# Five more block products by seven multiplications in an fp32 two-layer network: q·G in the first attention, the out projection in the second

## The chip, the cores and the metric

One Trainium2 chip, one core of it. The time is device microseconds (us) of one execution. The kernel before takes 990.49 us, the median of 3 runs (990.44 to 990.85). The profile is of one further execution, which took 988.88 us.

## The reference

Two transformer layers in fp32, for a batch of 2 sequences of 1024 tokens with 512 channels; a layernorm with a residual stands around each of the four parts.

```
# layer 0, linear attention: q, k = elu(x W) + 1; v = x Wv
out = einsum('bhtd,bhde,bht->bhte', q, k^T v, 1 / (q . sum k))
x   = layernorm(x + out @ Wo.T)
# layer 0, feed-forward: weights of 4 bits, unpacked and scaled; y / rms(y)
x   = layernorm(x + ffn4(x))
# layer 1, gated linear attention, 16 heads that share q and k
go  = o @ Wog.T + x @ Wig.T
o   = o * rsqrt(mean(o*o)) * g_norm_w * (go * sigmoid(go))
x   = layernorm(x + o @ Wo.T)
# layer 1: a router takes the top 512 of each 1024 tokens, an MLP adds to these
x   = layernorm(scatter_add(x, top, sigmoid(score) * mlp(x[top])))
```

The first attention is computed as x + q·G, where q already carries the weight 1/(q · sum k), and G (512 x 512 for a sequence) is (kᵀx) Wv, masked to the heads, times Wo.

## The kernel before

**Tiling.** Tokens go in four blocks ("blk" 0 to 3) of 512; blocks 0 and 1 are sequence 0, blocks 2 and 3 sequence 1. A block is four row tiles of 128 tokens. Stages of the span: layer-0 attention 6.7 to 238 us, the 4-bit feed-forward 238 to 552, the gated attention 552 to 782, the routed MLP 789 to 972, then stores.

**Products by seven.** A block product of 512 x 512 by 512 x 512 is 16 matmuls of 128x512 if it is done whole. `by_seven` (L307) cuts both operands into 2 x 2 and needs seven products of half size (the Strassen-Winograd form), each of 4 matmuls of 128x256, with sums on VectorE: S1 = A21 + A22, S2 = S1 - A11, S3 = A11 - A21, and A12 - S2 of one operand; T1 to T4 of the other (`sums_of_weights`, L297). One PSUM bank, `grow`, takes product after product on top of one another, and a reader takes its value after each; the bank `side` does so for two. Before the change this form serves the projections q and k (L307), the gate of the second attention (`gate`, L1078) and the down products of the feed-forward (L679).

**Stage 1.** The loop `for b in range(B)` (L518) runs `run(products, *others)` (L490): the generator of seven products of the next projection, and between its steps lists of other steps: `add_xk` (kᵀx, L360), `values` and `G_rows` (L411, L427: G, copied from PSUM by VectorE and ScalarE in turn), `turned` (L434: the transposes of a row tile of q), `add_o` (L440), `unpack_some` (unpacks 4-bit weights on VectorE, L237 and L238) and `split_some` (L458: the split of x into a high and a low part for stage 2). `behind()` and `last_pe` pin TensorE's order to the order in which these steps are written; a scheduler orders the other engines' queues, each of which runs in order. `add_o(blk, i)` issues four matmuls of 128x512 into a bank, `ao` (L445), adds it to x (L453) and takes the row statistics (L188, L189); after the fourth row tile, GpSimd (POOL) applies the layernorm (L183). `weigh` (L396; L400 to L406) applies the weight to q, and is called from within `by_seven` through `ready`.

**Stage 3.** For each block, `attend` (L1016) computes o and the sums that gate's products need (L1056, L1057), `gate` computes go in seven products: (L1089), written from PSUM by ScalarE's copies and VectorE's adds, then Silu; the result is `u`, transposed, in a tile `uT` of its own for each block. `finish(blk - 1)` (L1123) is the out projection of the block before, 16 matmuls of 128x512 (L1133), four operations that add it to x, the row statistics, the layernorm and the router's scores (L1146). `route` turns the scores of a sequence into row numbers (L1163), and rows are fetched by them ("picked", "xs") for stage 4. TensorE's order in stage 3 is the scheduler's.

**The start.** L138 to L142 issue the loads of Wk on SP's DMA queue and of the first block of x transposed (`x0T`) on ScalarE's queue, the first of them in small pieces (k = 0: three pieces of x0T, of 128, 128 and 256 columns, and two halves of Wk). The first projection (L474) multiplies them as they land.

Of the kernel before, what the change touches and what calls it, by code (L numbers as in the profile page):

```python
# [10 lines left out]
F32 = mybir.dt.float32  # L11
# [62 lines left out]
def body(ctx: ExitStack, tc: tile.TileContext, a: dict, out: bass.AP):  # L74
# [63 lines left out]
    for k in range(KC):  # L138
        for half in ((slice(0, 256), slice(256, 512)) if k == 0 else (slice(0, 512),)):
            nc.sync.dma_start(out=Wk[:, k, half], in_=a["WkT"][k * P : (k + 1) * P, half])  # L140
        for part in ((slice(0, 128), slice(128, 256), slice(256, 512)) if k == 0 else (slice(0, 512),)):
            nc.scalar.dma_start(out=t[:, k, part], in_=src[:, k, part])  # L142
# [154 lines left out]
    def sums_of_weights(w, rooms):  # L297

        B11, B12, B21, B22 = (w[:, 2 * e : 2 * e + 2, 256 * o : 256 * o + 256] for e in range(2) for o in range(2))
        T1, T2, T4 = rooms  # L300
        for dst, x, y in ((T1, B12, B11), (T2, B22, T1), (T4, B21, T2), (B12, B22, B12)):
            nc.vector.tensor_sub(dst, x, y)
        return T1, T2, B12, T4
# [91 lines left out]
    def weigh(blk, t):  # L395

        for r in range(2):
            x = pairs_of["q", blk][t][:, r]
            e = wk.tile([P, C], F32, tag="e", name="qk")
            nc.vector.tensor_mul(e, x, ksum_of[blk // 2])  # L400
            z = sp.tile([P, 16], F32, tag="z", name="z", bufs=2)
            nc.vector.tensor_reduce(z, e.rearrange("p (h d) -> p h d", d=32), AX.X, ALU.add)
            nc.vector.tensor_scalar_add(z, z, 1e-6)
            nc.vector.reciprocal(z, z)
            x3 = x.rearrange("p (h d) -> p h d", d=32)
            nc.vector.tensor_mul(x3, x3, z.unsqueeze(2).to_broadcast([P, 16, 32]))  # L406

    vkm_of, qT, parts = {}, {}, []
# [23 lines left out]

    def turned(blk, i):
        with behind():  # L434
            pt = transposed(pairs_of["q", blk][i // 2][:, i % 2], "qTp", acc_bank)
        last_pe[0] = last_turned[0]
        t = qT[blk, i] = wk.tile([P, KC, P], F32, tag="qT", name="qT")
        nc.scalar.copy(t.rearrange("p k t -> p (k t)"), pt)

    def add_o(blk, i):  # L440

        ao = acc_bank("ao")
        with behind():
            for k in range(KC):
                ins = nc.tensor.matmul(  # L445
                    ao, qT[blk, i][:, k], G_of[blk // 2][:, k], start=k == 0, stop=k == KC - 1
                ).ins
        last_pe[0] = ins
        x = x_t[blk][:, i]
        if i == 0:  # L450
            mv_of[blk] = sp.tile([P, 4, 2], F32, tag="mv", name="mv")
        mv = mv_of[blk]
        nc.vector.tensor_add(x, ao, x)  # L453
        row_stats(mv[:, i], x)
        if i == 3 and blk < NB - 1:
            layernorm(x_t[blk], mv, by=nc.gpsimd)
# [48 lines left out]
    def some_o(blk, *part):  # L505
        return [lambda i=i: add_o(blk, i) for i in part]
# [6 lines left out]
    def q_products(blk):  # L513
        return by_seven(xT[blk], Wq, Ts["q"], S_rooms, pairs_of.setdefault(("q", blk), []), lambda t: weigh(blk, t))

    step = lambda f, *x: [lambda: f(*x)]

    for b in range(B):  # L518
        i, j = 2 * b, 2 * b + 1
        if b:  # L520
            run(
                k_products(i),
                turns(1, 0, 1),
                some_o(1, 0) + turns(1, 2) + job(1) + some_o(1, 1) + turns(1, 3) + job(1),
                some_o(1, 2) + job(1), some_o(1, 3) + job(1), job(2),
            )
# [3 lines left out]
        else:  # L530
# [7 lines left out]
            q_products(i), [],  # L538
            some_xk(j, 0, 1) + job(1), some_xk(j, 2) + step(spread_ksum, b) + job(1), some_xk(j, 3) + job(1 + b),
        )  # L540
        if b == 0:
# [4 lines left out]
            q_products(j),  # L546
            step(values, b),
            turns(i, 0, 1) + job(1 - b),
            step(G_rows, b) + split[0] + job(1 - b),
            some_o(i, 0) + turns(i, 2) + split[1] + some_o(i, 1) + turns(i, 3) + job(1 - b),  # L550
            some_o(i, 2) + split[2] + some_o(i, 3),
# [3 lines left out]
    rings["free"] = rings["mm"]  # L555
    for more in turns(3, 0, 1) + split[3] + some_o(3, 0) + turns(3, 2) + some_o(3, 1) + turns(3, 3) + some_o(3, 2, 3):
        more()
# [496 lines left out]
    def other_sums(blk):  # L1054
        x, o = xT[blk], oT[blk]
        nc.vector.tensor_sub(x[:, :, 256:], o[:, :, 256:], x[:, :, 256:])  # L1056
        nc.vector.tensor_sub(T4, T2, o[:, :, :256])  # L1057

    banks = []
# [18 lines left out]
    def gate(blk):  # L1078

        u = uT[blk] = place_w(3, "uT")  # L1080
# [4 lines left out]
        def product(w, b, half):  # L1085
            ps = acc_bank("go")
            for m in range(2):
                for k in range(KC):
                    nc.tensor.matmul(  # L1089
                        ps[:, 256 * m : 256 * m + 256],  # L1090
                        w[:, k, m],
                        b[:, k, 256 * half : 256 * half + 256],
                        start=k == 0,
                        stop=k == KC - 1,
                    )
            return ps.rearrange("p (m t) -> p m t", m=2)

        def end(e):
            half = u.rearrange("p (m e) t -> p m e t", e=2)[:, :, e]
            nc.scalar.activation(half, half, AF.Silu)  # L1100
            for m in range(2):
                f = 2 * m + e
                ins = nc.vector.scalar_tensor_tensor(
                    u[:, f], oT[blk][:, f], gw[:, f : f + 1], u[:, f], ALU.mult, ALU.mult
                ).ins
            return ins

        nc.scalar.copy(c11, product(gA11, x, 0))
        yield
        nc.scalar.copy(c22, product(gS1, T1, 0))  # L1110
        yield
        p2 = product(gA12, oT[blk], 0)
        nc.vector.tensor_add(c12, c11, product(gS2, T2, 0))
        yield nc.vector.tensor_add(c11, c11, p2).ins
        nc.vector.tensor_add(c21, c12, product(gS3, x, 1))
        nc.vector.tensor_add(c12, c12, c22)
        yield nc.vector.tensor_add(c22, c22, c21).ins
        nc.vector.tensor_add(c12, c12, product(gS4, oT[blk], 1))
        yield end(0)
        nc.vector.tensor_sub(c21, c21, product(gA22, T4, 0))  # L1120
        yield end(1)

    def finish(blk):  # L1123

        mv = sp.tile([P, 4, 2], F32, tag="mv", name="mv")
# [3 lines left out]
        if blk == 3:  # L1129
            steps = [(0, 0), (0, 1), (1, 0), (1, 1), (0, 2), (0, 3), (1, 2), (1, 3)] + steps[8:]  # L1130
        for i, n in steps:
            k = (0, 2, 1, 3)[n]
            nc.tensor.matmul(ao[i], uT[blk][:, k, i * P : (i + 1) * P], W1o[:, k], start=n == 0, stop=n == 3)  # L1133
# [4 lines left out]
        power = layernorm(x_t[blk], mv)  # L1138
# [8 lines left out]
        return power, ins  # L1147
# [304 lines left out]
    for blk in range(NB):  # L1452
        sum2 = attend(blk)
        if blk == 0:
            plain_gate(0, False)
        else:
            o_sum(blk)
            _, scored = finish(blk - 1)
            gating = gate(blk)
            for _ in range(2):  # L1460
                next(gating)
# [123 lines left out]
```

## Time and profile before

| what | value |
|---|---|
| median of the runs | 990.49 us (990.44 to 990.85) |
| the profiled execution | 988.88 us |
| its span | 987.1 us |
| granted TensorE clock, mean | 0.998 |
| DMA | 48.84 MB, mean 49 GB/s |

The profile follows one execution from its first to its last instruction, the span. PE is TensorE's matmuls, PEld its weight loads, DVE VectorE, ACT ScalarE, POOL GpSimd, SP the engine whose DMA queue takes most loads. A matmul in fp32 leaves two records. A row of the kind `L445 PE ao<-G,qT 128x512 x128 | 57.3, 593` gives line, engine, output and inputs by the program's names, shape, number of records, busy time in us, and the mean duration of one in ns; the records of neighbouring matmuls overlap, so what a matmul takes is read from a run of them on the chain of waits. The list of waits names the line of an engine that stood idle, what released it, and us in total, times, and the longest. In a timeline the first two numbers are start and duration in us.

### The profile page before, as it was taken

What the parts mean: (1) busy time and instruction counts of PE and PEld (TensorE: products, weight loads), DVE (VectorE), ACT (ScalarE), POOL (GpSimd) and SP (SyncE); (2) the same over time, 40 slices, a digit from 0 to 9 for tenths busy, and PEclk for the clock granted to TensorE, in tenths of its full rate; (3) what the DMA queues carried; (4) which work ended last, traced back from release to release, by engine and by line L of the source; (5) the groups of instructions that cost most, each with busy time, mean ns of one, the idle gap of its engine ahead of it and who ended that gap; (6) DMA issues with size and microseconds to landing.
All of it is one profiled execution on the core that took longest, in us unless ns stands there. A gap on an engine that the chain in (4) does not pass through costs nothing.

```text
span 987.1 us, 11453 instructions
## 1 busy us (share of the span) xinstructions
PE 972.1 (98%) x4253; PEld 745.1 (75%) x4253; DVE 683.3 (69%) x1291; ACT 288.4 (29%) x490; POOL 300.2 (30%) x276
## 2 busy tenths in 40 slices
PE   9999999999999999999999999999999999999996
PEld 6667666756888888888889655776768688888885
DVE  3568877867975686686672465466798795789644
ACT  2244333333542272263240432132220123220000
POOL 1110452004887265575565022002032011000022
PEclk9999999999999999999999999999999999999999
DMA  9632212100000000000020500000004302140011
GB/s 332 200 91 79 72 53 93 37 0 1 1 1 1 1 1 0 2 11 1 1 86 1 220 4 1 1 1 1 1 33 139 128 17 70 43 171 1 1 43 43
DMA packets 25979, 48.84 MB, mean 49 GB/s; under 512 B 4685, under 2 KB 6733, under 8 KB 25412
## 3 DMA queue, kind: packets, MB, share of 16 engines
q1 hardware_dynamic: 23139, 42.85, 13.1%
q0 software_dynamic: 1920, 4.22, 1.1%
q10 hardware_dynamic: 864, 1.05, 0.3%
q8 instruction: 33, 0.54, 0.2%
q14 instruction: 23, 0.18, 0.1%
HBM read 39.70 MB, written 10.52 MB: 51 GB/s over the span
## 4 chain that ended last, share of the span: by engine, by line
PE 84%; issue 8%; DVE 4%; POOL 2%; ACT 1%; DMA 1%; POOLq 0%; ACTq 0%; DVEq 0%
PE P L679 12%; PE yp L1329 9%; PE hp L1250 9%; PE gatep L632 8%; PE upp L632 8%; PE ao L445 6%; PE xk L367 6%; PE grow L316 5%; PE P L316 4%; PE ao L1133 3%; PE go L1089 2%; PE lp L595 1%; PE P L688 1%; PE kp L474 1%; PE up L1006 1%
## 5 line engine op out<-in xcount | busy, mean ns | idle before, releaser
L181 POOL TENSOR_TENSOR rs<-rs,table 128x4 f32<-128x4 f32 (+1 forms) x21 | 18.9, 902 | 327.9 <-DVE rs L180 327.6
L643 DVE SCALAR_TENSOR_TENSOR gate<-gatep,scale,gate 128x512 f32<-128x512 f32 x123 | 91.4, 743 | 7.4 <-PE gatep L632 6.9
L643 DVE SCALAR_TENSOR_TENSOR up<-upp,scale,up 128x512 f32<-128x512 f32 x112 | 83.1, 742 | 0.2
L632 PE MATMUL gatep<-x1Th,wgu 128*128 128x512 f32 x176 | 72.7, 413 | 0.0
L632 PE MATMUL upp<-x1Th,wgu 128*128 128x512 f32 x176 | 69.7, 396 | 0.0
L632 PE MATMUL gatep<-x1Tl,wgu 128*128 128x512 f32 x176 | 69.6, 395 | 0.0
L632 PE MATMUL upp<-x1Tl,wgu 128*128 128x512 f32 x176 | 69.5, 395 | 0.0
L679 PE MATMUL P<-wdn,h 128*128 128x256 f32 x256 | 60.5, 379 | 0.0
L832 POOL TENSOR_TENSOR h<-up,gate 128x512 f32<-128x512 f32 x30 | 38.6, 1287 | 70.4 <-ACT gate L831 65.3
L637 ACT ACTIVATE gate<-gatep,scale 128x512 f32<-128x512 f32 x41 | 28.3, 691 | 106.8 <-PE gatep L632 106.8
L445 PE MATMUL ao<-G,qT 128*128 128x512 f32 x128 | 57.3, 593 | 0.0
L1133 PE MATMUL ao<-W1o,uT 128*128 128x512 f32 x128 | 55.6, 592 | 0.0
L679 PEld LDWEIGHTS P<-wdn,h 128*128 128x128 f32 x256 | 48.5, 190 | 6.7
L1037 POOL TENSOR_TENSOR sum<-sum,sq 128x512 f32<-128x512 f32 x12 | 18.2, 1517 | 107.6 <-issue 83.7
L1133 PEld LDWEIGHTS ao<-W1o,uT 128*128 128x128 f32 x128 | 24.0, 190 | 28.7 <-issue 27.5
L188 DVE BATCH_NORM_STATS2 st<-x 128x6 f32<-128x512 f32 x64 | 42.7, 682 | 0.8
L367 PE MATMUL xk<-pair,x 128*128 128x512 f32 x96 | 42.7, 592 | 0.0
L445 PEld LDWEIGHTS ao<-G,qT 128*128 128x128 f32 x128 | 23.8, 190 | 24.3 <-issue 23.9
L632 PEld LDWEIGHTS upp<-x1Th,wgu 128*128 128x128 f32 x176 | 33.0, 188 | 9.3 <-DVE up L643 1.1
L632 PEld LDWEIGHTS upp<-x1Tl,wgu 128*128 128x128 f32 x176 | 33.1, 188 | 7.6
L632 PEld LDWEIGHTS gatep<-x1Th,wgu 128*128 128x128 f32 x176 | 33.1, 188 | 7.4 <-issue 0.3
L632 PEld LDWEIGHTS gatep<-x1Tl,wgu 128*128 128x128 f32 x176 | 33.1, 188 | 7.1
(405 smaller groups left out, 2239.5 us busy)
## 6 DMA issues: line engine op xcount, KB each, us to landing
pk<-in_gu SPq DMA_DIRECT2D x16, 352.0 KB, 3.7
x<-in_x SPq DMA_DIRECT2D x4, 1024.0 KB, 13.1
w<-in_w SPq DMA_DIRECT2D x1, 4096.0 KB, 16.1
xs<-picked SPq DMA_DIRECT2D x4, 1024.0 KB, 5.0
out<-x SPq DMA_DIRECT2D x4, 1024.0 KB, 4.3
w<-in_w SPq DMA_DIRECT2D x4, 1024.0 KB, 6.3
x0T<-in_xT SPq DMA_DIRECT2D x3, 1024.0 KB, 7.2
pk<-in_dn SPq DMA_DIRECT2D x11, 256.0 KB, 3.3
```

Source lines behind the costliest of these rows:

```text
L188: nc.vector.bn_stats(st, x)
L316: ins = nc.tensor.matmul(ps[:, 256 * r : 256 * r + 256], a[:, k, r * P : (r + 1) * P], b[:, k], start=first and r == 0 and k == 0, stop=k ...
L367: ins = nc.tensor.matmul(acc_of[b][c], x_t[blk][:, i, c * P : (c + 1) * P], pairs_of["k", blk][i // 2][:, i % 2], start=blk % 2 == 0 and i ...
L445: ins = nc.tensor.matmul(ao, qT[blk, i][:, k], G_of[blk // 2][:, k], start=k == 0, stop=k == KC - 1).ins
L632: ins = nc.tensor.matmul(ps, wgu[:, k, at * P : (at + 1) * P], x[:, k], start=x is parts[0], stop=x is parts[1]).ins
L637: nc.scalar.activation(acc, ps, AF.Copy, scale=s)
L643: last = nc.vector.scalar_tensor_tensor(acc, ps, s, acc, ALU.mult, ALU.add).ins
L679: last_p[0] = nc.tensor.matmul(cut, x(j)[:, r], w[:, j], start=j == 0, stop=j == NP - 1 and tail is None).ins
L832: hm = nc.gpsimd.tensor_mul(h.chunk(f), up, gate).ins
L1133: nc.tensor.matmul(ao[i], uT[blk][:, k, i * P : (i + 1) * P], W1o[:, k], start=n == 0, stop=n == 3)
L1250: nc.tensor.matmul(ps[:, 256 * j : 256 * j + 256], w[:, k, 2 * g + j], x[:, k], start=k == 0, stop=k == 1)
L1329: nc.tensor.matmul(ps[:, 256 * r : 256 * r + 256], x(r, j), w(j), start=j == 0, stop=j == NJ - 1)
```

## The change

1. q·G of blocks 0, 1 and 2 goes by seven products (`o_products`), in place of four `add_o`; block 3 stays whole (`whole_o`). q transposed is one tile for a block. The sums of G are made in `G_rows`, for each sequence. Each product is added to x by VectorE; `grow` takes four products and `side` two. The row statistics and POOL's layernorm come behind the last product.
2. In `run`, q's and k's products are interleaved with the new steps in another distribution; `weigh` of the second block of a sequence is no longer called by `by_seven` but placed among the steps; the four splits of block 0 are spread over q(3)'s products.
3. The out projection of blocks 0 and 1 in stage 3 goes by seven products (`finish_by_seven`), interleaved with gate's products; blocks 2 and 3 stay with `finish`. The sums of its weight are made once (`sums_of_W1o`), those of u for each block (`sums_of_u`). `scored_rows` holds what came after the out projection.
4. `gate` lets its products accumulate in PSUM, in two banks, in place of four of VectorE's adds, and ScalarE copies or applies Silu straight from the bank; all blocks share one `uT`, and TensorE's order there is pinned by `last_3`.
5. The third piece of x0T at the start is issued on SP's queue.

The diff, cut to its core:

```diff
-            nc.scalar.dma_start(out=t[:, k, part], in_=src[:, k, part])
+            (nc.sync if part.start == 256 else nc.scalar).dma_start(out=t[:, k, part], in_=src[:, k, part])
...
     def G_rows(b):
...
+        TG[b] = sums_of_weights(G_of[b], rooms), pieces_of(room[:, 3])
...
+    def o_products(blk):
+
+        A11, A12, A21, A22 = (qT[blk][:, 2 * e : 2 * e + 2, 256 * t : 256 * t + 256] for t in range(2) for e in range(2))
+        G = G_of[blk // 2]
+        B11, _, B21, B22 = (G[:, 2 * e : 2 * e + 2, 256 * o : 256 * o + 256] for e in range(2) for o in range(2))
+        (T1, T2, T3, T4), S1 = TG[blk // 2]
+        S2 = pieces_of(wk.tile([P, 512], F32, tag="qS", name="qS", bufs=1))
+
+        def product(ps, a, b, first, t, o):
+
+            with behind():
+                for r in range(2):
+                    for k in range(2):
+                        ins = nc.tensor.matmul(
+                            ps[:, 256 * r : 256 * r + 256], a[:, k, r * P : (r + 1) * P], b[:, k],
+                            start=first and r == 0 and k == 0, stop=k == 1, skip_group_check=True,
+                        ).ins
+            last_pe[0] = ins
+            x = x_t[blk][:, 2 * t : 2 * t + 2, 256 * o : 256 * o + 256]
+            nc.vector.tensor_add(x, x, ps.rearrange("p (r c) -> p r c", r=2))
+
+        nc.vector.tensor_add(S1, A21, A22)
+        nc.vector.tensor_sub(S2, S1, A11)
+        nc.vector.tensor_sub(A21, A11, A21)
+        grow = acc_bank("grow")
+        product(grow, A11, B11, True, 0, 0)
+        yield
+        product(acc_bank("P2"), A12, B21, True, 0, 0)
+        yield
+        product(grow, S2, T2, False, 1, 0)
+        nc.vector.tensor_sub(A12, A12, S2)
+        yield
+        side = acc_bank("P7")
+        product(side, A21, T3, True, 1, 1)
+        yield
+        product(grow, S1, T1, False, 1, 1)
+        yield
+        product(side, A22, T4, False, 1, 0)
+        yield
+        product(grow, A12, B22, False, 0, 1)
+        yield
+        mv = mv_of[blk] = sp.tile([P, 4, 2], F32, tag="mv", name="mv")
+        with tc.issue_after(weighed[0]):
+            for i in range(4):
+                row_stats(mv[:, i], x_t[blk][:, i])
+            layernorm(x_t[blk], mv, by=nc.gpsimd)
+        yield
...
         if b:
             run(
                 k_products(i),
-                turns(1, 0, 1),
-                some_o(1, 0) + turns(1, 2) + job(1) + some_o(1, 1) + turns(1, 3) + job(1),
-                some_o(1, 2) + job(1), some_o(1, 3) + job(1), job(2),
+                turns(1, 0, 1) + job(1), job(1),
+                turns(1, 2, 3) + some_o(1, 1) + job(1), some_o(1, 2) + job(1), some_o(1, 5) + job(1),
             )
...
         run(
-            q_products(j),
+            q_products(j, lambda t: None),
             step(values, b),
-            turns(i, 0, 1) + job(1 - b),
-            step(G_rows, b) + split[0] + job(1 - b),
-            some_o(i, 0) + turns(i, 2) + split[1] + some_o(i, 1) + turns(i, 3) + job(1 - b),
-            some_o(i, 2) + split[2] + some_o(i, 3),
+            turns(i, 0, 1) + split[0] + job(1 - b),
+            step(G_rows, b) + split[1] + turns(i, 2, 3) + job(1 - b),
+            some_o(i, 2) + split[2] + some_o(i, 1) + job(1 - b),
+            step(all_free) + some_o(i, 1) + step(weigh, j, 0) + split[3] + some_o(i, 3) + step(weigh, j, 1) + some_o(i, 1),
         )
...
     def gate(blk):
...
-        nc.scalar.copy(c11, product(gA11, x, 0))
-        yield
-        nc.scalar.copy(c22, product(gS1, T1, 0))
-        yield
-        p2 = product(gA12, oT[blk], 0)
-        nc.vector.tensor_add(c12, c11, product(gS2, T2, 0))
+        one, two = acc_bank("go"), acc_bank("go")
+        nc.scalar.copy(c11, product(one, gA11, x, 0, True))
+        yield
+        p5 = product(two, gS1, T1, 0, True)
+        yield
+        nc.scalar.copy(c22, p5)
+        yield
+        nc.scalar.copy(c12, product(one, gS2, T2, 0, False))
+        p2 = product(acc_bank("go"), gA12, oT[blk], 0, True)
         yield nc.vector.tensor_add(c11, c11, p2).ins
-        nc.vector.tensor_add(c21, c12, product(gS3, x, 1))
-        nc.vector.tensor_add(c12, c12, c22)
-        yield nc.vector.tensor_add(c22, c22, c21).ins
-        nc.vector.tensor_add(c12, c12, product(gS4, oT[blk], 1))
+        p7 = product(one, gS3, x, 1, False)
+        yield nc.vector.tensor_add(c22, c22, p7).ins
+        nc.vector.tensor_add(c12, c12, product(two, gS4, oT[blk], 1, False))
         yield end(0)
-        nc.vector.tensor_sub(c21, c21, product(gA22, T4, 0))
+        nc.scalar.activation(c21, product(one, gA22, T4, 0, False), AF.Silu)
+        nc.scalar.activation(c22, c22, AF.Silu)
         yield end(1)
...
+    def finish_by_seven(blk, u, w):
+
+        (A11, A12, A21, A22), (S1, S2) = u
+        (B11, B21, B22), (T1, T2, T3, T4) = w
+
+        def product(ps, a, b, first, s, o):
+
+            with tc.issue_after(last_3[0]) if last_3[0] else contextlib.nullcontext():
...
+            last_3[0] = ins
+            for r in range(2):
+                i = 2 * s + r
+                x = x_t[blk][:, i, 256 * o : 256 * o + 256]
+                nc.vector.scalar_tensor_tensor(
+                    x, ps[:, 256 * r : 256 * r + 256], inv[blk][:, i : i + 1], x, ALU.mult, ALU.add
+                )
...
-            _, scored = finish(blk - 1)
             gating = gate(blk)
-            for _ in range(2):
-                next(gating)
+            if blk < 3:
+                finishing = finish_by_seven(blk - 1, sums, W1o_sums)
+                for _ in range(2):
+                    next(finishing)
+                    next(gating)
+                next(finishing)
+                scored = scored_rows(blk - 1)
+            else:
+                scored = finish(blk - 1)
+                for _ in range(2):
+                    next(gating)
+            next(gating)
```

## The prediction

> **What bounds the kernel now.** I read the page first: the busy shares, the tenths and the chain that ended last by engine.
>
> ```profile
> span 987.1 us, 11453 instructions
> PE 972.1 (98%) x4253; PEld 745.1 (75%) x4253; DVE 683.3 (69%) x1291; ACT 288.4 (29%) x490; POOL 300.2 (30%) x276
> PE   9999999999999999999999999999999999999996
> DVE  3568877867975686686672465466798795789644
> PE 84%; issue 8%; DVE 4%; POOL 2%; ACT 1%; DMA 1%; POOLq 0%; ACTq 0%; DVEq 0%
> ```
>
> TensorE is busy in 98% of the span, in every slice but the last. It is idle for 987.1 - 972.1 = 15 us, most of it at the start and the end. Second, what TensorE waits for, the whole list:
>
> ```profile
> PE dp L989 <- DVE last L974: 1.5, 2, 1.2
> PE ep L942 <- ACT l L931: 1.3, 1, 1.3
> PE hp L1250 <- ACT row L1218: 1.1, 1, 1.1
> PE idle L285 <- DVE ones L281: 1.0, 1, 1.0
> PE rp L1163 <- DVE score L1146: 0.9, 1, 0.9
> PE kp L474 <- DMA x0T<-in_xT: 0.3, 1, 0.3
> PE mp L1043 <- POOL sum L1037: 0.3, 1, 0.3
> ```
>
> That is 6.4 us in all. No bank that `by_seven` fills (`grow`, `P`) is in it: products that accumulate into one bank, with a reader in between, cost TensorE nothing today. So a saved matmul saves its own time, as far as the other engines keep up. Third, therefore, the stretches that the change touches, cut out as windows: q·G of blocks 0 and 1, q·G of block 2 with the splits, and the out projections of blocks 0 and 1. Columns: length, then busy time of PE, PEld, DVE, ACT, POOL, granted clock, DMA share, GB/s.
>
> ```profile
> 84.50:133.50 49.00, 49.00 (x173) 30.44 (x172) 38.55 (x78) 19.34 (x31) 10.75 (x6) 1.00 0.22 66
> 184.40:238.20 53.80, 53.80 (x219) 34.19 (x217) 39.66 (x84) 18.36 (x31) 8.63 (x5) 1.00 0.00 1
> 612.60:643.00 30.40, 30.40 (x155) 21.92 (x154) 15.69 (x29) 5.59 (x9) 4.65 (x4) 1.00 0.00 1
> 673.60:710.00 36.40, 36.40 (x139) 23.95 (x138) 25.34 (x46) 6.49 (x11) 6.14 (x5) 1.00 0.00 1
> ```
>
> PE is full in all four at full clock; VectorE is idle for 10.4, 14.1, 14.7 and 11.1 us. The spare VectorE time is what the change spends.
>
> **1. Five blocks in seven products.** From the chain, one `by_seven` product and one whole out projection; from the groups, a weight load of such a product:
>
> ```profile
> 97.51 1.73 PE P L316 x8
> ```
>
> ```profile
> 612.74 13.73 PE ao L1133 x32
> ```
>
> ```profile
> L316 PEld LDWEIGHTS P<-Wq,b 128*128 128x128 f32 x32 | 6.1, 190 | 0.8
> ```
>
> A matmul leaves two records. 32 records of 512 columns take 13.73 us (0.429 each); a 256-column product takes 8 records, 1.73 us (0.216 each). Whole: 13.73. Seven products: 7 x 1.73 = 12.09 (1.727 unrounded). Saved: 1.64 a block, and for the three q·G and two out projections **-8.2 us**. The order of instructions says the same: 80 matmuls of 512 columns fewer, 140 of 256 more.
>
> A rule speaks against it: the Trainium skill, "TensorE: Matmul & The Clock Gate", The mechanism, has it that a weight load overlaps matmuls in flight only where its row group differs. These loads fill the array, and a block goes from 32 to 56 of them. In series, a block would cost 56 x (0.190 + 0.216) = 22.7 instead of 32 x (0.190 + 0.429) = 19.8 us: +2.9, so +14.6 in five. But the row has eight records with eight loads of 0.190 in 1.73 us, which leaves no room for a load in series: the loads are hidden. The measurement decides: -8.2.
>
> **2. VectorE in q·G of blocks 0 and 1.** An operation of 512 elements lasts 0.68 us and follows the last at 0.60. Each block gains 3 sums of q, one A12 - S2 and 7 adds of products, and loses 4 adds (L453): 7 x 0.60 = +4.2. The four sums of G add 2.4. Two blocks: +10.8. The four row statistics of block 1 (2.8) now come behind its last add. So, until that add, 38.55 + 10.8 - 2.8 = 46.6 us of work; 0.8 of it can't be closed up, where VectorE waits for ScalarE's exponentials. VectorE ends at 84.5 + 47.4 = 131.9. TensorE alone would end at 133.5 - 2 x 1.64 = 130.2. VectorE becomes the bound by 1.7 and a hand-over of 0.2: **+1.9**. By place: the third product needs S2, which stands behind the copies and sums of G (0.5); the third product of block 1 likewise (0.9); a continuation on `side` (0.5). Queued behind a waiting product are the next products of q, for TensorE's order is pinned. Bounds: 0 (the scheduler's order hides all) to 3.3 (all taken back).
>
> Does POOL slow these sums? The layernorm of block 0 (L183, 9.5 us) now runs beside the three sums of block 1.
>
> ```profile
> 116.62 0.97 DVE L238 TENSOR_SCALAR pk<-pk 128x704 int32<-128x704 int32 x1
> ...
> 121.89 0.68 DVE L340 TENSOR_TENSOR rw<-x0T,rw 128x512 f32<-128x512 f32 x1
> ```
>
> ```profile
> 614.53 2.29 DVE L1056 TENSOR_TENSOR x2T<-oT,x2T 128x1024 f32<-128x1024 f32 x1
> ```
>
> Both of the first run beside L183. The Trainium skill, "GPSIMD Engine Reference", Specifications, says that VectorE contends with GpSimd where it has two SBUF inputs. L1056 bears it out beside L1037 (2.29; its like L1057 alone has 1.21), L340 doesn't beside L183 (0.68, as always; the integer L238 takes 0.97 for 0.52). By the rule three sums take about 0.6 more each and the two blocks save 1.8 us less; by L340 nothing. The sums are L340's kind beside the same POOL instruction: nothing, with 1.8 in the range.
>
> **3. q·G of block 2, the splits and block 3.** VectorE: 39.66 + 4.2 + 2.4 = 46.3 us of work in 53.8 - 1.6 = 52.2: it fits. Spots remain where split 3's copies and the last product come close: **+0.4** (0 to 1.5). The layernorm of block 2 starts after its last product; the first gate/up matmuls need only the splits of block 0, so its cover is stage 2. Moving `weigh` out of q's products costs nothing while VectorE has this room; `all_free` only opens banks earlier.
>
> **4. Out projection and gate, blocks 0 and 1.** VectorE per block: 14 operations of 128x256 at 0.40 (L1375's kind, 0.48 long) for 4 of 512, 14 x 0.40 - 4 x 0.60 = +3.2, and 4 sums, +2.4; W1o's sums, +2.4 once; four gate adds fewer in each of three blocks, -2.4 each. Two blocks and W1o: 11.2 + 2.4 - 4.8 = +8.8, against 14.7 + 11.1 us idle. ScalarE takes the copies and Silu straight from PSUM, with idle 24.8 and 29.9 of the windows. A continuation waits for VectorE to read the bank: 0.2 to start, 0.69, 0.15 back, 1.04 us, under the 1.73 of the product in between; here gate's products stand in between too. I take **+0.3** (0 to 1.5). W1o lands at 557.3 (5.5 us after its issue); by the order of instructions its sums stand in VectorE's queue where it is at 558.3, 50 us ahead of their use. That is 1.0 us of cover: later than that, all of VectorE's queue, attention's first operations, would wait with them. The scores of block 1 come later behind the row statistics, but what is fetched by them landed at 748.7 and is first used at 764.5: 16 us of cover, so nothing; without it, `rp L1163` (0.9) would grow by the delay of about 2.
>
> **5. The load.** The third piece of the first xT, 128 x 256 values, went third on ScalarE's queue (issued at 1.64, landed at 6.69; TensorE waits 0.3 for it at 6.73). On SP's queue it is third too, behind two halves of Wk: 0, with -0.3 to +0.3. All that SP issues behind it (three more pieces of Wk, x, the next xT, the shift, the table) comes one small load later; no wait in the list is for one of these, and ScalarE's own later pieces come one earlier.
>
> Sum: -8.2 + 1.9 + 0.4 + 0.3 + 0 = **-5.6 us**. The profiled execution took 988.88 (span 987.1 and 1.78 around it), so span 981.5 and 983.3; the median of the runs, 990.49, is 1.61 above the profiled one, so 984.9.
>
> **The rivals.**
> B: VectorE's order hides everything but 0.6: 990.49 - 7.6 = 982.9. For it: before, no product waits for VectorE, and by the windows three of four stretches have room. Against: 47.4 us of work for 45.7.
> C: VectorE takes back most: POOL's slowing (1.8) and the upper bounds of parts 3 and 4 in halves (1.7 more): -2.1, 988.4. For: the VectorE row has 8s and 9s there already. Against: L340.
> D, slower: a ping-pong between TensorE and VectorE. All 20 continuations on a PSUM bank (four in each of five blocks) wait for an add, the add behind q queued VectorE operations: 1.04 + 0.60 q - 1.73 each. It decides where a continuation costs over 8.2 / 20 = 0.41, at q = 1.8. At q = 2.5: 20 x 0.81 = 16.2, net +8.0: 998.5. Against: `by_seven` has three such continuations in every block and none waits; and where VectorE isn't full, such queues don't stand. The windows have it idle for a fifth to a half.
> E: the change doesn't do what it says, as the loads aren't hidden: 990.49 + 14.6 = 1005.1; excluded by the 1.73 us row.
>
> **How the numbers follow.** A measurement of this kernel tells about 0.2% (2.0 us) from no change. A (the sum, 983.5 to 986.8) has 0.54, B 0.22, C 0.17 (986.8 to 991), D 0.06, E 0.01. Faster than 988.5: A, B and half of C, 0.84; within: the rest of C, 0.09; slower: 0.07. The range runs from 982.0 (all of 8.2 kept and 0.3 of the load) to 989.0; D, E and a part of C, about 0.15, are left out.
>
> **What would show it.** Right: q·G and out products at 1.73 with loads of 190 ns; new waits of TensorE for VectorE's S2 and on `grow` or P7 in stage 1, about 2 us; VectorE without gaps from about 85 to 132; stage 1 ending some 2.5 us earlier, the stretch with the out projections 3 us. Wrong: products of 256 columns above 1.73; waits on each continuation, in stage 3 too; sums of over 1 us beside L183; a longer wait for xT at the start; or a new wait for the scores or for the rows fetched by them.

## The result and the profile after

The changed kernel takes 985.68 us, the median of 6 runs (984.94 to 985.81), against 990.47 (989.04 to 990.85, 6 runs) before: ratio 0.9953, 95% interval 0.994 to 0.9965, so 4.8 us or 0.47% faster. The forecast was 984.9 with a range of 982.0 to 989.0.

```profile
PE 967.1 (98%) x4373; PEld 768.5 (78%) x4373; DVE 697.6 (71%) x1340; ACT 290.3 (30%) x496; POOL 302.9 (31%) x276
```

By the two profiled executions the gain is only 987.1 - 983.8 = 3.3 us. Of the 1.5 us between this and 4.8, 0.8 lie in the first 20 us: TensorE reaches the second block's first product (`grow L316`) at 18.86 us in the profile of before and at 19.64 in that of after, and this differs from execution to execution, as the first experiment shows.

```profile
18.86 1.89 PE L316 MATMUL grow<-Wk,x0T 128*128 128x256 f32 x8
```

```profile
19.64 1.89 PE L316 MATMUL grow<-Wk,x0T 128*128 128x256 f32 x8
```

From that product to the end of the span the two take 968.24 and 964.16 us: **4.08 us less**. This time, from that product to the end of the span, is called the "rest" below and given for every kernel; it can be read to 0.1 us. The remaining 0.7 between 4.08 and the medians' 4.8 can't be placed, as only one execution of each kernel has a profile.

What TensorE waits for, in the profile of after (total, times, longest):

```profile
PE ep L1008 <- ACT l L997: 1.8, 2, 1.3
...
PE gatep L698 <- DVE x1Tl L212: 0.6, 1, 0.6
PE up L1072 <- DVE decay L1057: 0.4, 1, 0.4
PE x2Tp L197 <- ACT e L1009: 0.4, 1, 0.4
...
PE grow L462 <- DVE x L468: 0.3, 1, 0.3
```

Against the list of before, `ep` has a second wait of 0.5, and the other four lines are new. One is in q·G of block 0 (`grow`), one at the entry into stage 2 (`gatep`), three in stage 3. Where the saved 8.2 us went is read by taking the same TensorE work in both traces and asking how much earlier it starts, with the start of the rest set equal:

| stretch | saved on TensorE | seen in the traces | taken back | predicted |
|---|---|---|---|---|
| q·G of blocks 0 and 1 (to the next k product, 133.52 and 131.71) | 3.28 | 2.59 | 0.7 | 1.9 |
| block 2, splits, entry into stage 2 (to stage 2's first products `P`) | 1.64 | -0.23 | 1.9 | 0.4 |
| stage 3 (to `hp`, 780.0 before) | 3.28 | 1.71 | 1.6 | 0.3 |
| all | 8.20 | 4.07 | 4.1 | 2.6 |

The time of a product is as forecast. Here are the weight loads of q·G, then three products from block 0's stretch, the middle one with S2 (columns: start, duration):

```profile
L462 PEld LDWEIGHTS P<-G,wdn 128*128 128x128 f32 x32 | 6.1, 190 | 0.8
```

```profile
91.25 1.89 PE L462 MATMUL P<-G,wdn 128*128 128x256 f32 x8
93.41 1.99 PE L462 MATMUL grow<-wdn,qS 128*128 128x256 f32 x8 [0.27 <-DVE x L468]
95.24 1.89 PE L316 MATMUL grow<-Wq,rw 128*128 128x256 f32 x8
```

Starts without a wait are 1.73 us apart (the printed duration includes the last matmul's tail), loads take 190 ns as before. The product with S2, block 0's third, starts 0.43 late (91.25 + 1.73 = 92.98), of which the list of waits has 0.27, and its successor another 0.10: here a stall costs more than its entry. It waits not for S2, which is done at 92.15, but for the add that reads `grow` after the first product and stands behind S2 in VectorE's queue:

```profile
92.67 0.69 DVE L468 TENSOR_TENSOR x<-x,grow 128x512 f32<-128x512 f32 x1
```

A second delay, of 0.18 with its successor's, at 103.96 (block 0's seventh product) is in no list. The stretch by busy time (length, PE, PEld, DVE, ACT, POOL):

```profile
84.50:131.70 47.20, 46.94 (x223) 39.80 (x222) 46.93 (x91) 20.07 (x33) 14.77 (x8) 1.00 0.25 74
```

VectorE is busy for 46.93 of 47.20 us: full, as forecast. At the entry into stage 2:

```profile
217.98 0.50 PE L698 MATMUL gatep<-x1Th,wgu 128*128 128x512 f32 x1 [0.57 <-DVE x1Tl L212]
...
240.54 0.50 PE L698 MATMUL gatep<-x1Th,wgu 128*128 128x512 f32 x1
...
241.20 0.50 PE L698 MATMUL upp<-x1Th,wgu 128*128 128x512 f32 x1
```

A pair of gate/up matmuls (high and low part) takes 0.47 us where nothing holds it; here two pairs start 0.66 apart, and VectorE's operations that empty their banks (L709) follow each other at 0.66 too. That lasts from 239.4 to 242.9 and costs about 1.2 us, in no line of the list.

### The profile page after: what moved, and what is told of

Read it like the earlier page. It is cut to its first block, busy times and chain, and to the rows that moved or that the text cites. A ratio compares the mean times of both kernels' runs of the same rounds, so it can differ in the third digit from the quotient of the medians.

```text
span 983.8 us, 11753 instructions
## 1 busy us (share of the span) xinstructions
PE 967.1 (98%) x4373; PEld 768.5 (78%) x4373; DVE 697.6 (71%) x1340; ACT 290.3 (30%) x496; POOL 302.9 (31%) x276
## 5 line engine op out<-in xcount | busy, mean ns | idle before, releaser
L181 POOL TENSOR_TENSOR rs<-rs,table 128x4 f32<-128x4 f32 (+1 forms) x21 | 20.3, 967 | 301.3 <-DVE rs L180 301.0
L709 DVE SCALAR_TENSOR_TENSOR gate<-gatep,scale,gate 128x512 f32<-128x512 f32 x123 | 91.5, 744 | 7.4 <-PE gatep L698 6.9
L709 DVE SCALAR_TENSOR_TENSOR up<-upp,scale,up 128x512 f32<-128x512 f32 x112 | 83.2, 743 | 0.2
L1463 PE MATMUL yp<-w,h 128*128 128x256 f32 x168 | 37.7, 379 | 0.0
L745 PE MATMUL P<-T,S 128*128 128x256 f32 x160 | 35.8, 379 | 0.0
L1463 PEld LDWEIGHTS yp<-w,h 128*128 128x128 f32 x168 | 31.9, 190 | 4.3
L1377 ACT ACTIVATE h<-h,b 128x512 f32<-128x512 f32 x28 | 18.4, 713 | 57.2 <-DVE h L1401 34.6
```

Of the source, the lines that this page charges most:

```text
L181: power = nc.gpsimd.tensor_tensor(rs[:, :n], rs[:, :n], const("mhalf")[:, :n], ALU.pow).ins
L709: last = nc.vector.scalar_tensor_tensor(acc, ps, s, acc, ALU.mult, ALU.add).ins
L745: last_p[0] = nc.tensor.matmul(cut, x(j)[:, r], w[:, j], start=j == 0, stop=j == NP - 1 and tail is None).ins
L1377: nc.scalar.activation(x, x, AF.Gelu_apprx_tanh, bias=b1[:, f : f + 1])
L1463: nc.tensor.matmul(ps[:, 256 * r : 256 * r + 256], x(r, j), w(j), start=j == 0, stop=j == NJ - 1)
```

## The experiments

Each kernel is given with its rest, from `grow L316`'s first start to the end of the span (before 968.24, changed 964.16).

### The load at the start

```diff
 # before, with:
-            nc.scalar.dma_start(out=t[:, k, part], in_=src[:, k, part])
+            (nc.sync if part.start == 256 else nc.scalar).dma_start(...)
```

> The kernel before with only the third piece of x0T moved to SP's queue. The prediction put this at 0 (-0.3 to +0.3). Theory M, from the two traces: TensorE enters the second block's products 0.78 us later (19.64 for 18.86), so the move costs about 0.8 us: 991.3 for 990.5. Rival L: the start differs from execution to execution (the profiled execution of before was 1.6 us under its median, and the change is 4.8 us by the medians but 3.3 by the spans), and the move makes the common case better: 989.0 or less.

Measured 989.55 us against 989.93 (27 runs) for before, ratio 0.9994 (0.9986 to 1.0003). The start is at 19.44, the rest 968.26.

> The changed kernel with the third piece of x0T back on ScalarE's queue. Theory M: 0.8 us less than the changed kernel, 984.9. Rival L: more than the changed kernel, 986.4 or above. By the prediction: the same 985.7.

Measured 985.85 us, ratio to before 0.9954 (0.9941 to 0.9968); start 19.95, rest 964.15. So the move is worth nothing that can be measured, as predicted; theory M took one execution's start for the kernel's, and L falls too. With the load back, and against this before of 27 runs, the medians give 985.85 - 989.93 = -4.08, as the rest does. In the four profiles with the piece on ScalarE's queue the start lies at 18.86, 19.63, 19.95 and 20.50; in the ten with it on SP's (the changed kernel's among them) between 19.44 and 20.32. The first projection shows two causes. These lines are from the profile of before, then from that of the kernel with stage 3 alone changed (below), then from that of the changed kernel:

```profile
4.51 1.89 PE L474 MATMUL kp<-Wk,x0T 128*128 128x256 f32 x8
6.73 12.29 PE L474 MATMUL kp<-Wk,x0T 128*128 128x256 f32 x32 [0.33 <-DMA x0T<-in_xT]
```

```profile
4.61 2.94 PE L474 MATMUL kp<-Wk,x0T 128*128 128x256 f32 x8
8.37 12.29 PE L474 MATMUL kp<-Wk,x0T 128*128 128x256 f32 x32 [0.81 <-DMA x0T<-in_xT]
```

```profile
4.61 15.19 PE L528 MATMUL kp<-Wk,x0T 128*128 128x256 f32 x40
```

In the second, the load's arrival moved by 1.6 us with neither a change to it nor to anything ahead of it, and the start with it. In the third TensorE doesn't wait for the load: its first eight records take 3.0 us (4.61 to 7.61) where they take 1.7 before, and the next 32 follow at once. So the start hangs on the load in some executions and on TensorE's slow first records in others; why these are slow was not tested.

### Stage 1 alone, stage 3 alone

```diff
 # e3: the changed kernel, with the load and everything from other_sums on
 #     (gate, finish, stage 3's loop) as before
 # e4: before, with everything from other_sums on as in the changed kernel
```

> Stage 1 of the change alone (three blocks of q.G by seven, the splits, weigh moved), the load and stage 3 as before. The saved TensorE time is 3 x 1.64 = 4.9 us. By the prediction VectorE takes back 1.9 in blocks 0 and 1 and 0.4 in block 2: -2.6. By the traces, 0.7 in blocks 0 and 1 and 1.9 in block 2 with the entry into stage 2: -2.3, 988.2. If the parts don't add (stage 3 works only on what stage 1 leaves), it differs from -2.3 by more than 0.5.

Measured 987.19 us, ratio 0.997 (0.9958 to 0.9982); start 19.63, rest 965.87: -2.37.

> Stage 3 of the change alone (two out projections by seven, gate accumulating in PSUM), stage 1 and the load as before. Saved TensorE time 3.3 us. By the prediction 0.3 is taken back: -3.0, 987.5. By the traces 1.6 is taken back, by waits of TensorE for ScalarE's l and e and for VectorE's decay: -1.7, 988.8.

Measured 988.42 us, ratio 0.9982 (0.9974 to 0.999); start 20.50, rest 966.5: -1.74. The two add to -4.11, the whole is -4.08 (and by the medians -4.08 for the changed kernel with the load back): the parts don't disturb each other, and the table above holds for each alone. This start, by itself, hides all of stage 3's gain in e4's span (987.0 against 987.1).

### Block 2 whole again

```diff
-            some_o(i, 2) + split[2] + some_o(i, 1) + job(1 - b),
-            step(all_free) + some_o(i, 1) + step(weigh, j, 0) + split[3] + some_o(i, 3) + step(weigh, j, 1) + some_o(i, 1),
+            o_steps(i, 0) + split[2] + o_steps(i, 1) + job(1 - b),
+            step(all_free) + o_steps(i, 2) + step(weigh, j, 0) + split[3] + o_steps(i, 3) + step(weigh, j, 1) + o_steps(i, 4),
 # for block 2, o_steps gives add_o's row tiles (0, 1), (2,), (), (3,), ()
 # and POOL's layernorm; G_rows makes no sums of G for it
```

> The changed kernel with q.G of block 2 whole again (16 matmuls of 512), its steps at the places of the seven products; blocks 0 and 1, the splits, weigh and stage 3 as changed. Measured from the start of the second block's first product (the start itself differs by up to 1.6 us between executions): the changed kernel has 964.16 us from there to the end of the span. Theory M: block 2's products cost VectorE 6.6 us where stage 2's evictions of gate and up need it, and give back 1.87 of their 1.64; without them 963.9 (-0.2), and TensorE's pairs of gate and up no longer go at 0.66 us. Rival R: the 1.87 comes of the splits and weigh in their new places; then whole costs 1.64 more, 965.8.

Rest 967.04: 2.9 us more than the changed kernel. M falls. R's 1.64 is exceeded as well: TensorE has new waits for VectorE (0.9 at `x1Tp`, 0.7 at `qTp`), and the pairs at 242.7 to 245.4 still go at 0.66 to 0.73. So in this order of steps the seven products of block 2 do save their time, and the loss at the entry into stage 2 doesn't come of their adds alone: it is there without them.

### The first gate/up matmuls behind block 3

```diff
-                    with ExitStack() if ins is None else tc.issue_after(ins):
+                    with tc.issue_after(last_pe[0] if ins is None else ins):
                         for x in parts:
```

> The changed kernel with the first gate/up matmul of stage 2 issued behind block 3's last q.G product on TensorE; in the changed kernel three pairs of them (1.4 us) stand before or between block 3's products. Measured from the second block's first product to the end of the span (964.16 us in the changed kernel). Theory G: the 1.87 us that block 2 and the entry into stage 2 give back come of this order: TensorE stands 0.57 (with hand-over 0.8) for the split's last low part, and the pairs done early delay block 3's last add, behind which VectorE then evicts gate and up at 0.66 us a pair where TensorE has 0.47 (about 1.2 us). With the pairs behind, both go: 962.3, and the pairs at 239 to 243 us go at 0.47. Rival H: VectorE's work is what it is, the entry stays bound by VectorE, and only the first wait goes: 963.4; or TensorE has nothing else at 217 us and nothing is gained: 964.2.

Rest 964.77, 0.6 more by the spans, 0.40 by the shift of equal TensorE work. G falls. The slow pairs are gone, as G had it, but other waits stand in their place (TensorE in this kernel):

```profile
218.99 1.99 PE L462 MATMUL grow<-G,qT 128*128 128x256 f32 x8 [1.28 <-DVE x L468]
...
221.99 0.66 PE L197 MATMUL qTp<-table,pair 128*128 128x128 f32 x4 [0.57 <-DVE x L468]
```

In the changed kernel three pairs were done while TensorE would have waited here. The loss keeps about its size (1.28 + 0.57 and their hand-overs for 0.57 and 1.2), wherever the order puts it. That fits a loss set by VectorE's work behind q(3)'s last products, but no run lightens that work alone. In the changed kernel, VectorE stands idle just ahead of it:

```profile
211.31 0.69 DVE L273 SCALAR_TENSOR_TENSOR pair<-grow,e 128x512 f32<-128x512 f32 x1 [2.15 <-ACT e L272]
```

It waits 2.15 us for the exponential of q(3)'s product and then has work without a gap until 228.6: the weights of q, the last split, block 2's adds and statistics.

### VectorE in q·G of blocks 0 and 1

```diff
         nc.vector.tensor_sub(S2, S1, A11)
-        nc.vector.tensor_sub(A21, A11, A21)
...
         product(acc_bank("P2"), A12, B21, True, 0, 0)
+        nc.vector.tensor_sub(A21, A11, A21)
         yield
 # and in gate:
-        nc.scalar.copy(c12, product(one, gS2, T2, 0, False))
+        (nc.vector.tensor_copy if blk == 1 else nc.scalar.copy)(c12, product(one, gS2, T2, 0, False))
```

> The changed kernel with two small edits at places far apart. First, in the three q.G blocks by seven, the sum A21' = A11 - A21 is issued behind the second product in place of ahead of the first: it then stands behind, not ahead of, the add of the first product in VectorE's queue. Theory O: TensorE's wait of 0.43 at the third product of block 0 is for that add, and goes, with its 0.1 behind: 0.5 gained before 100 us; rival D (VectorE's total work bounds the stretch): the wait turns up at the next product, nothing gained by 132 us. Second, gate's copy c12 on VectorE in block 1 alone: 1.2 us gained by 665 us, as in the run with it in all blocks, and nothing given back in blocks 2 and 3. Both: 962.4 from the second block's first product to the end, 964.16 in the changed kernel.

TensorE in the stretch:

```profile
92.88 1.89 PE L462 MATMUL grow<-wdn,qS 128*128 128x256 f32 x8
...
103.86 1.99 PE L462 MATMUL grow<-G,wdn 128*128 128x256 f32 x8 [0.45 <-DVE x L468]
```

The third product no longer waits, and the seventh starts 0.61 late in place of 0.08. The two losses are equal, 0.71 with the successors', so by 132 us nothing is gained: theory D, VectorE's throughput. The second edit is read in the stage-3 section below. Rest 962.96.

```diff
-            turns(i, 0, 1) + split[0] + job(1 - b),
-            step(G_rows, b) + split[1] + turns(i, 2, 3) + job(1 - b),
-            some_o(i, 2) + split[2] + some_o(i, 1) + job(1 - b),
+            turns(i, 0, 1) + split[0],
+            step(G_rows, b) + split[1] + turns(i, 2, 3),
+            some_o(i, 2) + split[2] + some_o(i, 1),
 # and in k(j)'s run:
-        some_xk(i, 3) + job(1), job(1 + b))
+        some_xk(i, 3) + job(1), job(1 + 4 * b))
```

> The changed kernel with three unpacking jobs (two VectorE operations of 0.5 us each and a load) moved from q(1)'s products, where q.G of block 0 begins, into k(3)'s. The work of VectorE ahead of the third product of block 0 falls by up to 3 us. Theory D (the prediction's step 2: the waits there are VectorE's throughput): TensorE's waits at S2 of block 0 and behind it, 0.7 us in all, are gone: 963.5 (964.16 in the changed kernel). Rival O: they are a matter of one operation's place or of hand-over: less than 0.3 gained.

Rest 972.03, 7.9 us more: neither D nor O is tested cleanly. In the stretch itself the delays grew from 0.7 to 1.75 us (0.41 at the third product, 1.34 at the sixth and seventh), as the scheduler put the next block's sums into the freed places. Most of the loss comes later. VectorE in this kernel:

```profile
176.74 0.49 DVE L237 TENSOR_SCALAR pk<-pk,shift 128x512 int32<-128x512 int32 x1 [1.72 <-DMA pk<-in_dn]
...
186.42 0.68 DVE L344 TENSOR_TENSOR pair<-pair,P 128x512 f32<-128x512 f32 x1
```

The later jobs all shift, and their first operations wait at the head of VectorE's queue for loads (5 us between 170 and 185, this one 1.72). q's `pair` stands behind them, and TensorE waits 3.4 us for it at `P L316`. Unpacking is cover only as long as its load has landed. The wait is followed by a slower clock; TensorE, then the busy times from 187.3 to 190.7 (the number behind POOL's is the granted clock):

```profile
187.15 3.63 PE L316 MATMUL P<-Tq,x0T 128*128 128x256 f32 x8 [3.43 <-DVE pair L344]
```

```profile
187.30:190.70 3.40, 3.40 (x9) 2.69 (x10) 2.86 (x7) 2.69 (x5) 0.00 (x0) 0.51 0.50 120
```

The granted clock is 0.51 in these 3.4 us, and the product takes 3.43 us to its successor's start in place of 1.73: another 1.7 of the 7.9 us.

> The changed kernel with two sums of q (A21' and A12 - S2) on POOL in blocks 0 and 2, where POOL is idle, and with gate's copy c12 on VectorE in block 1. VectorE has 1.2 us less in each of the two q.G stretches, where TensorE lost 0.7 and 1.9 us in the changed kernel. Theory D (VectorE's throughput bounds both stretches): up to 0.7 gained by 132 us and about 1 by 300 us, as less VectorE work lets each later add come earlier. Rival O: in block 2 TensorE waits for the last operations behind q's last products, where these sums have long been done: 0.7 by 132 us, and nothing more by 300 us. Rival P: VectorE's sums with two inputs in SBUF are held up by POOL's: operations of 0.69 us become 1 us and more, and nothing is gained or some lost. With c12's 1.25 at block 1: 961.2 (D), 962.2 (O) or 962.9 and more (P) from the second block's first product to the end, 964.16 in the changed kernel; a median of about 983 to 984.5, so faster than both kernels.

```diff
-        nc.vector.tensor_sub(A21, A11, A21)
+        by = nc.vector if blk == 1 else nc.gpsimd
+        by.tensor_sub(A21, A11, A21)
...
-        nc.vector.tensor_sub(A12, A12, S2)
+        by.tensor_sub(A12, A12, S2)
 # and c12 on VectorE in block 1, as in the kernel with A21' moved
```

Measured 986.78 us (5 runs), ratio to before 0.9965 (0.9952 to 0.9979): slower than the changed kernel. Rest 964.82, 0.7 more. With c12's gain of 1.26, which is there, the sums on POOL cost 1.9 us. P holds. VectorE, then POOL, in block 0:

```profile
91.81 1.39 DVE L471 TENSOR_TENSOR qS<-wdn 128x512 f32<-128x512 f32 x1
...
93.72 1.67 DVE L323 TENSOR_TENSOR Tk<-x0T 128x512 f32<-128x512 f32 x1
```

```profile
91.37 1.28 POOL L473 TENSOR_TENSOR wdn<-wdn 128x512 f32<-128x512 f32 x1 [34.73 <-DVE wdn L470]
```

S2 and the next projection's first sum take 1.39 and 1.67 for 0.69, just where POOL's two sums run (the second from 93.57 to 94.84): VectorE loses 1.7 us for the 1.2 it was spared. S2, and behind it the first product's add, hold the third product (0.5 late again), the sixth and seventh are late as well, and TensorE is 1.7 us further behind than in the changed kernel by the end of block 0. Block 2 adds only 0.1 to the loss: POOL's sums take 1.78 and 1.72 there and VectorE's 0.69. VectorE, then POOL, in block 2:

```profile
205.51 0.69 DVE L471 TENSOR_TENSOR qS<-TG,qT 128x512 f32<-128x512 f32 x1
```

```profile
205.55 1.78 POOL L473 TENSOR_TENSOR qT<-qT 128x512 f32<-128x512 f32 x1 [38.93 <-DVE TG L470]
```

In all four overlaps the operation that began first kept its time, and the other one ended late. So 1.2 us less work on VectorE ahead of q(3)'s last products gained nothing in block 2, as O has it.

### Stage 3: ScalarE's and VectorE's queues

```diff
-        nc.scalar.copy(c12, product(one, gS2, T2, 0, False))
+        nc.vector.tensor_copy(c12, product(one, gS2, T2, 0, False))
```

> The changed kernel with one copy of gate (c12, from PSUM) on VectorE in place of ScalarE. Theory Q: in block 1 ScalarE's exponential l waits 1.3 us in the queue behind this copy, which waits for TensorE; TensorE then waits 0.53 (and 0.2 of hand-over) for l. Without it: no second wait at ep for ScalarE's l, 963.4 from the second block's first product to the end (964.16 in the changed kernel). Rival V: VectorE is late there as well, through the scores; then 964.2.

Here c12 is on VectorE in all three blocks. ScalarE in the changed kernel, block 1, the copy and the exponential behind it:

```profile
643.48 0.59 ACT L1185 COPY uT<-go 128x512 f32<-128x512 f32 x1 [3.13 <-PE go L1156]
643.96 0.42 ACT L996 ACTIVATE l<-k 128x256 f32<-128x256 f32 x1
```

`l` is ready when VectorE's reciprocal ends at 642.67, and stands 1.3 us behind a copy that waits for TensorE. With the copy on VectorE, the state products (`up`) of block 2's attention start 1.26 us earlier, and TensorE's second waits at `ep` and `dp` are gone: Q. But `up` of block 3's attention then waits 2.15 for VectorE's decay, and `go` 1.2 for the copy itself: rest 967.95, +3.8. Behind the 2.15 the granted clock is 0.50 from 701.0 to 704.4, and `up`, `sc` and `sk` take 4.1 us there in place of 2.5, so 1.6 of the loss is the clock's. V holds for the other blocks. With c12 on VectorE in block 1 alone (the kernel with A21' moved, above) the 1.26 stays to the end. `ep` in the changed kernel, then in that one:

```profile
646.55 0.70 PE L1008 MATMUL ep<-l,table 128*128 128x256 f32 x2 [0.53 <-ACT l L997]
```

```profile
645.85 0.59 PE L1008 MATMUL ep<-l,table 128*128 128x256 f32 x2
```

Its rest is 962.96, 1.2 under the changed kernel and the shortest here (984.32 for its one execution).

> The changed kernel with the row statistics, layernorm and scores of blocks 0 and 1 (and the route behind them) issued after the next block's attention scores, in stage 3. Theory Q: in block 2 VectorE's kk, q and decay stand behind layernorm and scores, and TensorE waits 0.43 (and 0.3 of hand-over) for decay; with the order turned round the wait goes: 963.4 (964.16 in the changed kernel), and the rows fetched by the scores still arrive before they are used. Rival N: a new wait of about as much, of the route's transposes or of the fetched rows for the later scores: 964.2 or more.

```diff
                 next(finishing)
-                scored = scored_rows(blk - 1)
...
-        if blk == 2:
-            ranking = route(0, xT_tile("row"))
...
             scores(blk + 1, gates)
+        if 0 < blk < 3:
+            scored = scored_rows(blk - 1)
+        if blk == 2:
+            ranking = route(0, xT_tile("row"))
```

Rest 965.25. N holds: the wait for decay is gone, and `rp` has a second wait of 0.9 for the score; the pass of block 1 is 0.4 worse as well.

> The changed kernel with the statistics, layernorm and scores of block 1 alone issued behind block 3's attention scores, and the route's transposes one of gate's steps later, so that they don't wait for the scores. Theory Q: TensorE's wait for decay (0.43, 0.7 with its hand-over) goes and no other comes: 963.4 from the second block's first product to the end (964.16 in the changed kernel). Rival N: the later route delays the fetched rows or VectorE's ranking, and a wait of the same size turns up before 790 us: 964.2.

```diff
 # as above for block 2's pass alone, and the route's steps later:
-                    for _ in range((3, 2, 2, 3)[n]):
+                    for _ in range((0, 5, 2, 3)[n]):
```

TensorE's waits at `rp L1297` for the score are 1.8 us in two, as in the kernel above. Rest 964.88, and 0.46 lost just in this place: N again. The wait at `rp` came back although the transposes were issued a step later. In these orders either the next attention's chain or the route waits for VectorE. In the changed kernel, what holds `kk`, q and decay is a layernorm that itself waits for POOL:

```profile
696.11 1.92 DVE L183 TENSOR_SCALAR x<-x,mv,rs 128x512 f32<-128x512 f32 x4 [1.61 <-POOL rs L181]
```

Another order might serve both; none was found.

## Why the prediction was right, and where its steps were off

- **The saving of 8.2 us** is right: 1.73 us a product, 190 ns loads hidden, in both places. Rival E is out. The rule that it weighed does not hold for these loads: eight loads of 0.190 and eight matmul records go into each 1.73 us.
- **VectorE bounds q·G of blocks 0 and 1**: the mechanism is right (46.93 us busy of 47.20; in e10 the wait moves and doesn't go), the size is off: 0.7 for 1.9. The step that mis-sized it is "VectorE ends at 131.9 ... becomes the bound by 1.7": it made TensorE wait for VectorE's last add. VectorE's last add of block 1 in the changed kernel ends at 133.7, but the product behind it on TensorE starts at 131.71, in another bank. The backlog goes over into a stretch where VectorE has room (37.1 us busy of 52.3 from 131.7 on). Only an add that a continuation needs is waited for. The place was off too: the third product waits for the reader of `grow`, not for S2, and block 1's third doesn't wait at all. That banks of `by_seven` cost nothing before was weak evidence: ScalarE's copies empty its `grow`, while q·G's is emptied from VectorE's full queue.
- **POOL beside the sums**: "nothing" was right for these. In the changed kernel the three sums of block 1 take 0.69 us, beside L181 and L183, and POOL's L181 takes 2.47 for 1.04 there; A12 - S2 takes 1.05 beside L183, 0.36 more. Beside a POOL operation with two inputs it is different (e12, and L325 below).
- **Block 2 and the splits, "it fits", 0.4**: wrong by 1.5 us. The sum of the stretch (46.3 of 52.2) was no test, since the idle time lies ahead of q(3)'s last products, where VectorE waits 2.15 us for ScalarE (1.82 before), and the work comes behind them, up to the operations that empty stage 2's first banks. In e9 this loss only moves when the order of TensorE's work is changed. How it divides between the adds, `weigh` in its new place and the splits was not settled (e5 changes several at once).
- **Stage 3, 0.3**: wrong by 1.3 us. I counted VectorE's and ScalarE's idle time and the round trip to a bank, not what is queued behind an operation that waits. c12's copy on ScalarE holds `l`, shown by e6 and e10 (1.26 us, with the wait at `dp` behind it). Statistics, layernorm and scores, now later on VectorE, hold `kk`, q and decay: e7 and e11 remove that wait, and get one at `rp` for it, so this part of the loss, about 0.3, is seen and not won back by any run. That the scores' 16 us of cover for the fetched rows suffices was right.
- **The load**: 0, right (e1, e2). That TensorE's start differs by 1.6 us between executions I had not seen; it accounts for 0.8 of the 1.5 us by which the two profiles are closer than the medians.
- **Rival D of the prediction**, every continuation waits: out. Of the twelve continuations in stage 1 two were late, of the eight in stage 3 none.

So the sum was -5.6, and the same terms measured are -8.20 + 0.69 + 1.87 + 1.57 = -4.07. The errors of +1.2 and -2.8 partly cancel, which is luck; so is it that the medians' -4.8 lies nearer to the forecast than the mechanism's -4.1.

## What to carry to other kernels

Trading TensorE's time for VectorE's work pays when the freed time survives the queues: look at each added operation for what stands behind it in its engine's queue, and at idle time for whether it lies before or after the work, not at the sum of a stretch. Measure small gains from an event behind the start, when the start's loads vary by more than the gain. A wait that vanishes on a reorder and returns with the same length at a later operation points to an engine's throughput; one that goes and doesn't return (c12 in block 1) was an order. Look at the granted clock before a loss is put down to waits alone.

## What was not expected of the hardware

A POOL operation with two inputs from SBUF and VectorE's with two hinder each other: 1.39 and 1.67 us for 0.69 on VectorE in block 0 of e12, where POOL's began first; 1.78 and 1.72 for 1.28 on POOL in block 2, where VectorE's began first; 2.47 for 1.04 on POOL (L181 in the changed kernel). In the changed kernel VectorE's L325 began at 129.87 behind POOL's L386 (129.64):

```profile
129.87 1.75 DVE L325 TENSOR_TENSOR b<-x0T 128x512 f32<-128x512 f32 x1
```

Beside POOL's one-input L183, sums of VectorE took 0.69 in three cases and 1.05 in one.

After TensorE had waited 3.4 us (e8) and 2.15 us (e6), its granted clock was about half for 3.4 us. In the twelve other profiles TensorE has no wait above 1.3 us between 20 and 970 us, and the granted clock there is 1.00. Two cases don't show from which length of a wait on this happens.

TensorE's start moves by up to 1.6 us between executions of kernels that are alike up to there, with the landing of the first loads and with the pace of its first records.
